# A two-layer relational graph attention kernel: the elu's exponential written to PSUM in the first aggregation, and the scores' turn placed behind five parts of the product in the last

## The chip, the cores and the metric

The kernel runs on one core of a Trainium2 chip. The metric is device time in microseconds (us) from the start to the end of one launch. A core has five engines with one instruction stream each: TensorE (PE in the profile; PEld are its weight loads), VectorE (DVE), ScalarE (ACT), GpSimd (POOL) and SyncE (SP). An engine takes its own instructions in the order in which the program wrote them; between engines only semaphores order the work.

## The reference

Two layers of relational graph attention run over 3125 nodes of 768 features and 53,125 edges of 3 types; a residual and a LayerNorm close it. Cut to what matters:

```python
def rgat_conv(x, W, q, k, b, src, dst, etype, heads, out_ch, n_nodes):
    xr = jnp.einsum('nd,rdf->rnf', x, W)
    oi, oj = xr[etype, dst], xr[etype, src]
    alpha = jax.nn.leaky_relu(oi @ q + oj @ k, 0.2)
    e = jnp.exp(alpha - segment_max(alpha, dst)[dst])
    a = e / (segment_sum(e, dst)[dst] + 1e-16)
    msg = a[:, :, None] * oj.reshape(-1, heads, out_ch)
    return segment_sum(msg.reshape(-1, heads * out_ch), dst) + b

h = elu(rgat_conv(x, W1, q1, k1, b1, src, dst, etype, 4, 192, n))
out = layernorm(x + rgat_conv(h, W2, q2, k2, b2, src, dst, etype, 1, 768, n))
```

elu(v) is max(v, 0) + min(exp(v), 1) - 1.

## The kernel before, in words

Edges are sorted by destination. The 3125 nodes make 25 blocks of up to 128; a block owns 17 slots of 128 edges (block 0 has 14). One slot is one gather: an indirect DMA that POOL issues (L485) and that brings 128 rows of 772 numbers from the table `ftab` in device memory into one row of a ring in SBUF. An aggregation makes 422 of them.

There are three stages. Phase 1 multiplies the nodes by the weights of layer 1 and writes the table. Phase 2 is the first aggregation (4 heads): scores (`alpha`), their transposition on PE, maxima by scans and exponentials, weighted sums of the rows on PE into PSUM, then `e_y`, `e_x`, `e_h` (the elu), the transposition of h (`e_t`, into the PSUM tile `pt`, the two "turning banks"), and the dense products of layer 2 (`po`), which refill the table. Phase 3 is the last aggregation (one head): for each block

- `a_alpha` (DVE L1309 to L1315) adds the rows' keys and the queries to scores `al`; it needs the block's last gathered row;
- `a_turn` turns `al` and `next` on PE into the bank `pa`;
- `a_scan` (DVE L1326, L1328, L1331) finds the maxima, `a_exp` (ACT L1335) takes the exponential, `a_back` turns it back on PE;
- `weigh` (DVE L1359, four instructions) multiplies the marks by it, and `sums` (8 groups on PE, into `acc`) adds the weighted rows;
- of the block before, the `r_` steps bring the sums together (`r_plus`, DVE L1420, two halves), and the product `D` by one relation's second weights runs on PE in 12 parts: six of 512 columns, then six of 256. LayerNorm and the store close it.

The order is not found by a scheduler. Both phases put each step into a list with a key, in units of one gather (17 of them are a block), sort the list, and call the steps in that order; so the keys decide what stands in front of what on each engine. `STEPS3["s"]` holds, counted from the unit e at which the block's gathers are issued: alpha, turn, scan, exp, back, weigh, sums. `STEPS3["r"]` holds the `r_` steps (the last two are the halves of `r_plus`), `STEPS3["d"]` the 12 parts. Two steps occur once, behind the last gather: for the last block the product runs in a split precision, and its weights are split there, `w2_high` (ACT L1427, six casts) and `w2_low` (DVE L1431, six subtractions), with keys 6.0 to 6.51 units after the last block's e, alternating:

```python
for t in range(DT):
    when(NK + 6 + 0.1 * t, w2_high, t)
    when(NK + 6.01 + 0.1 * t, w2_low, t)
```

In phase 2 the elu works on a 128x768 tile: `e_x` (ACT L1026) writes the exponential to `ey`, `e_h` (DVE L1063) clips it, and L1065 and L1066 add max(y, 0) to it.

Of the kernel before, what the change touches and what calls it, by code (L numbers as in the profile page):

```python
# [9 lines left out]
F32 = mybir.dt.float32  # L10
# [11 lines left out]
P = 128  # L22
# [43 lines left out]
def _index(ap):  # L66
# [36 lines left out]
STEPS3 = {"f": -13,  # L103
          "marks": -5,
          "q": (-19, -17.27, -3.5, -2),
          "s": (1.9, 3.0, 3.05, 3.1, 5.6, 5.7, 9.5),
          "round": 0.9,
          "r": (16.7, 16.7, 16.72, 16.75, 19.25, 19.3, 16.71, 16.73, 20.5, 20.6),
          "t": (16.74, 16.78),
          "d": ((19.5, 22.5, 7), (22.8, 26.2, 5)),  # L110
          "y": (26.6, 26.7, 26.8, 29.5, 29.6),
# [4 lines left out]
def kernel(  # L116
# [31 lines left out]
    F1 = D // H1  # L148
# [695 lines left out]
    def phase2(work, psum):  # L844
# [177 lines left out]

        def e_x(b):
            s = blk[b]
            s["ey"] = work.tile([P, 4, F1], F32, name="ey", bufs=1)
            S.activation(s["ey"], s["y"][:, :, :F1], AF.Exp)  # L1026

        def busy(n):
# [117 lines left out]
        for b in range(NB):  # L1146
            at_0 = base(b + 1) - SL
            when(max(at_0 + STEPS2["marks"], 0.5), marks, b)
            for u, name in enumerate(("first", "second")):
                when(max(at_0 + STEPS2["f"][u], 0.1 + 0.1 * u), f_load, b, u)  # L1150
                for d, f in zip(STEPS2[name], (alpha, turn, scan, back, weigh, sums)):
                    if b > 0:
                        when(at_0 + d, f, b, u)
                if b == 0:
                    for d, f in zip(STEPS2["second0" if u else name], (alpha, turn, scan, back, weigh, sums)):
                        if u == 1 or f is not sums:
                            when(d, f, b, u)
                    if u == 0:
                        for i, d in enumerate(STEPS2["sums0"]):
                            when(d, sums, b, u, i)  # L1160
            for d, f in zip(STEPS2["h"], (e_y, e_x, e_h, h_row, e_t, e_s, e_s2)):
                when(at_0 + d, f, b)
            n = 0
            for i, (a, e, m) in enumerate(STEPS2["d"]):
                for j in range(m):
                    when(at_0 + a + (e - a) * j / m, d_part, b)
                    n += 1
                    for p in range(4):
                        if n == 18 * (p + 1):
                            when(at_0 + a + (e - a) * j / m + STEPS2["copy"], d_row, b, p)  # L1170
                            when(at_0 + a + (e - a) * j / m + STEPS2["tail"], d_tail, b, p)
            assert n == 72
# [431 lines left out]
    with tc.manual_schedule():  # L1604
        with tc.tile_pool(name="share", bufs=1) as pool:
# [5 lines left out]
            with tc.tile_pool(name="wbuf", bufs=1) as wbuf:  # L1611
                weights[0] = [wbuf.tile([P, DT, WA], F32R, name=f"wa{s}") for s in "HL"]
                with tc.tile_pool(name="wrest", bufs=1) as wrest, tc.tile_pool(name="pre", bufs=1) as pre:
# [16 lines left out]
                    with tc.tile_pool(name="work0", bufs=1) as work, tc.tile_pool(  # L1630
                        name="psum0", bufs=1, space=PSUM
# [23 lines left out]
                    with tc.tile_pool(name="work1", bufs=1) as work, tc.tile_pool(  # L1655
                        name="psum1", bufs=1, space=PSUM
# [3 lines left out]
                with tc.tile_pool(name="exbuf", bufs=1) as exbuf:  # L1660
                    extra = exbuf.tile([P, NX, RW], F32, name="extra")
                    with tc.tile_pool(name="work2", bufs=1) as work, tc.tile_pool(
                        name="psum2", bufs=1, space=PSUM
                    ) as psum:
                        phase2(work, psum)
                    with tc.tile_pool(name="work3", bufs=1) as work, tc.tile_pool(
                        name="psum3", bufs=1, space=PSUM
# [545 lines left out]
```

## Time and profile before

| | us |
|---|---|
| median of 3 runs | 1728.38 |
| lowest, highest | 1726.51, 1731.38 |
| the profiled execution's own time | 1726.83 |
| its span in the profile | 1724.9 |
| phase 3's gathers, first start to last start | 1131.84 to 1681.86 |

Busy shares of the span: PE 95%, DVE 64%, POOL 52%, ACT 25%. They are averages over three stages with different limits, so the stages have to be read one by one: which engine has no idle time there, and what ended the idle time of the others. In a row of a timeline the first number is the start in us from the start of the span, the second the duration, and the bracket gives the idle time just before it and what ended it; rows that are alike and follow one another are put together with their count. PE's instructions overlap, so a duration of a group is less than the sum of its members.

### The profile page before, as it was taken

The page shows a single profiled execution, that of the slowest core. Times are in us where ns is not written, and L with a number is a line of the kernel's source. Part 1 is how long each engine was busy: PE and PEld are TensorE (multiplying, and loading weights), DVE is VectorE, ACT ScalarE, POOL GpSimd, SP SyncE. Part 2 cuts the span into 40 slices and gives each one's busy share as a digit, 9 for nine tenths or more (in the row PEclk, how much of TensorE's full clock was granted, in tenths as well). Part 3 has the DMA queues.
Part 4 walks back from the last instruction along what each step waited for, and adds up shares of the span by engine and source line. Part 5 has one row for each costly group of instructions (what it writes and reads, how often), then busy time and mean ns, then how long its engine had stood idle before and what let it go on. Part 6 is the DMA issues. An engine that isn't in the chain of part 4 may idle for free.

```text
span 1724.9 us, 39077 instructions
## 1 busy us (share of the span) xinstructions
PE 1640.5 (95%) x14233; PEld 1269.5 (74%) x14233; DVE 1106.6 (64%) x4107; ACT 423.8 (25%) x796; POOL 904.8 (52%) x907
## 2 busy tenths in 40 slices
PE   9999999999996999999999999939999999999996
PEld 8999999999995788888888888924444444444443
DVE  5467666676425566666677777465766666666665
ACT  5122222112110111111111111212333333333333
POOL 5100000000007777777777777057777777777770
PEclk9999999999997999999999999969999999999999
DMA  9576766666568999999999999569999999999991
GB/s 329 180 244 210 258 220 210 199 183 203 191 251 281 330 345 355 347 348 348 346 346 356 354 351 351 172 230 324 334 336 340 335 337 338 338 336 340 334 338 39
DMA packets 169368, 500.48 MB, mean 290 GB/s; under 512 B 39891, under 2 KB 82490, under 8 KB 169167
## 3 DMA queue, kind: packets, MB, share of 16 engines
q0 software_dynamic: 70832, 343.91, 56.1%
q1 hardware_dynamic: 90104, 143.89, 25.0%
q10 hardware_dynamic: 8230, 10.10, 1.7%
q8 instruction: 114, 1.87, 0.4%
q14 instruction: 88, 0.71, 0.1%
HBM read 412.96 MB, written 89.63 MB: 291 GB/s over the span
## 4 chain that ended last, share of the span: by engine, by line
PE 69%; DMA 12%; issue 8%; POOL 6%; DVE 4%; ACT 0%; POOLq 0%; DVEq 0%; ACTq 0%; SPq 0%
PE po L56 47%; PE acc L56 13%; PE D L56 4%; DMA waH<-ftab,ridx 3%; DMA waL<-ftab,ridx 3%; POOL waH L485 2%; PE pa L59 2%; PE pt L59 2%; DMA share<-ftab,ridx 1%; DMA extra<-ftab,ridx 1%; POOL waL L485 1%; POOL extra L485 1%; DMA spare_rows<-ftab,ridx 1%; POOL share L485 1%; PE bank L56 1%
## 5 line engine op out<-in xcount | busy, mean ns | idle before, releaser
L485 POOL DMA_INDIRECT extra<-ftab,ridx x296 | 303.3, 1025 | 90.2 <-issue 48.2
L56 PE MATMUL po<-waH,hT 128*128 128x386 f32 (+1 forms) x1200 | 323.1, 344 | 1.0 <-DVE hT L1055 0.8
L56 PE MATMUL po<-waH,xT 128*128 128x386 f32 x1104 | 293.0, 341 | 0.0
L485 POOL DMA_INDIRECT share<-ftab,ridx x209 | 214.2, 1025 | 63.7 <-issue 36.3
L56 PEld LDWEIGHTS po<-waH,hT 128*128 128x128 f32 x1200 | 220.4, 189 | 3.4 <-DVE hT L1055 1.1
L56 PE MATMUL po<-waL,hT 128*128 128x386 f32 (+1 forms) x600 | 207.6, 346 | 0.0
L56 PE MATMUL D<-extra,AT 128*128 128x512 f32 (+1 forms) x576 | 207.2, 503 | 0.0
L56 PEld LDWEIGHTS po<-waH,xT 128*128 128x128 f32 x1104 | 202.4, 189 | 0.5 <-issue 0.4
L56 PE MATMUL po<-waL,xT 128*128 128x386 f32 x552 | 186.9, 339 | 0.0
L598 ACT COPY share<-po 128x386 f32<-128x386 f32 x150 | 72.3, 482 | 371.2 <-PE po L56 298.7
L56 PEld LDWEIGHTS D<-extra,AT 128*128 128x128 f32 x576 | 105.6, 193 | 67.9 <-issue 60.3
L56 PE MATMUL acc<-waL,marks 128*32 128x386 f32 (+1 forms) x860 | 152.8, 490 | 0.0
L56 PE MATMUL po<-wbH,xT 128*128 128x386 f32 (+1 forms) x552 | 147.5, 341 | 1.3 <-DVE wbL L431 1.3
L56 PE MATMUL acc<-waH,marks 128*32 128x384 f32 (+1 forms) x828 | 141.3, 496 | 0.7 <-DVE marks L1359 0.7
L56 PE MATMUL acc<-extra,marks 128*32 128x386 f32 (+1 forms) x564 | 129.5, 487 | 0.0
L485 POOL DMA_INDIRECT waL<-ftab,ridx x108 | 108.1, 1001 | 32.9 <-issue 26.8
L56 PE MATMUL acc<-extra,sel 128*32 128x193 f32 x2736 | 122.6, 331 | 2.3 <-DVE sel L963 2.3
L927 ACT ACTIVATE e<-e 32x128 f32<-32x128 f32 (+2 forms) x50 | 15.5, 310 | 432.9 <-DVE e L926 432.9
L485 POOL DMA_INDIRECT waH<-ftab,ridx x103 | 102.8, 998 | 31.4 <-issue 25.0
L56 PEld LDWEIGHTS po<-waL,hT 128*128 128x128 f32 x600 | 113.7, 190 | 0.6 <-issue 0.3
L762 POOL DMA_DIRECT2D share<-in_L_gnn_W_dram x24 | 12.8, 536 | 188.4 <-DVE w2j L773 117.3
L56 PEld LDWEIGHTS acc<-extra,sel 128*32 128x32 f32 x2736 | 86.7, 111 | 31.4 <-issue 5.8
(312 smaller groups left out, 3078.1 us busy)
## 6 DMA issues: line engine op xcount, KB each, us to landing
ftab<-share SPq DMA_DIRECT2D x150, 193.0 KB
ftab<-r SPq DMA_DIRECT2D x50, 386.0 KB
sT<-dr_d SPq DMA_DIRECT2D x23, 544.0 KB
xb_d<-share SPq DMA_DIRECT2D x25, 384.0 KB
ftab<-y SPq DMA_DIRECT2D x100, 96.0 KB
share<-xb_d SPq DMA_DIRECT2D x25, 384.0 KB
share<-in_x_dram SPq DMA_DIRECT2D x24, 384.0 KB
out_dram<-share SPq DMA_DIRECT2D x24, 384.0 KB
```

The costliest lines, as they stand in the source:

```text
L56: return self.add(self.engine.matmul(to, weights, moving, **more), to, moving)
L59: return self.add(self.engine.transpose(to, a, unit), to, a)
L485: return G.indirect_dma_start(out=to, out_offset=None, in_=tab, in_offset=_index(i[:, j:j + 1]), bounds_check=NP * R - 1, oob_is_err=False)
L598: S.copy(o[:, :HW], po[:, :HW])
L762: G.dma_start(w2[i][p:p + n], l2["W"][r, at:at + n, :])
L927: S.activation(e, e, AF.Exp)
```

## The change

Two edits. In phase 2 the exponential of the elu goes into a PSUM tile of the name that `e_t` uses a little later for h's transposition (`pt`, one buffer, two banks), where it was a tile in SBUF; the three DVE instructions of `e_h` then read it from there. In phase 3 the scores' steps get later keys: alpha 1.9 to 2.3, turn 3.0 to 4.3, scan and exp with it, back 5.6 to 6.5, weigh 5.7 to 6.6; the sums keep 9.5. The second half of `r_plus` moves from 20.6 to 21.37, which is 4.37 in the next block's units.

```diff
 STEPS3 = {...
-          "s": (1.9, 3.0, 3.05, 3.1, 5.6, 5.7, 9.5),
+          "s": (2.3, 4.3, 4.35, 4.4, 6.5, 6.6, 9.5),
           "round": 0.9,
-          "r": (16.7, 16.7, 16.72, 16.75, 19.25, 19.3, 16.71, 16.73, 20.5, 20.6),
+          "r": (16.7, 16.7, 16.72, 16.75, 19.25, 19.3, 16.71, 16.73, 20.5, 21.37),
...
         def e_x(b):
             s = blk[b]
-            s["ey"] = work.tile([P, 4, F1], F32, name="ey", bufs=1)
+            ey = psum.tile([P, 2, 512], F32, name="pt", bufs=1)
+            s["ey"] = ey.rearrange("p c (w f) -> p (c w) f", w=2)[:, :, :F1]
             S.activation(s["ey"], s["y"][:, :, :F1], AF.Exp)
```

The order of instructions changes in phase 3 alone, on PE and DVE; POOL, SP and ACT keep theirs. PE around the turn of the last block (every block has this pattern; `pa<-fident,al` and `pa<-fident,next` are the turn, `pa<-fident,e` the turn back, the D rows the parts of the product), before:

```order
L56 MATMUL D_14329<-extra,AT 128x512 x2
L59 MATMUL pa<-fident,al_0_14262 17x128
L59 MATMUL pa<-fident,next_14264 17x2x64
L56 MATMUL D_14329<-extra,AT 128x512 x4
L56 MATMUL D_14330<-extra,AT 128x256
L59 MATMUL pa<-fident,e 128x17
L56 MATMUL D_14330<-extra,AT 128x256 x5
L56 MATMUL acc_20486<-waL,marks 32x384 x2
```

and after:

```order
L56 MATMUL D_14329<-extra,AT 128x512 x5
L59 MATMUL pa<-fident,al_0_14262 17x128
L59 MATMUL pa<-fident,next_14264 17x2x64
L56 MATMUL D_14329<-extra,AT 128x512
L56 MATMUL D_14330<-extra,AT 128x256 x3
L59 MATMUL pa<-fident,e 128x17
L56 MATMUL D_14330<-extra,AT 128x256 x3
L56 MATMUL acc_20486<-waL,marks 32x384 x2
```

The turn stands behind five parts, not two; between it and the turn back there are now one part of 512 and three of 256, where there were four of 512 and one of 256; behind the turn back three are left of five.

DVE in the last block, behind the scores (the rows that go to share from acc are the halves of `r_plus`, marks from marks and pa is `weigh`, L1431 is `w2_low`), before:

```order
L1326 SCALAR_TENSOR_TENSOR F<-f,pa 17x256
L1328 SCALAR_TENSOR_TENSOR B<-f,F 17x192
L1331 TENSOR_TENSOR e<-pa,B 17x128
L1420 SCALAR_TENSOR_TENSOR share<-acc_20261,half,share 128x768
L1420 SCALAR_TENSOR_TENSOR share<-acc_20260,half,share 128x768
L1359 TENSOR_TENSOR marks<-marks,pa 128x544
L1359 TENSOR_TENSOR marks<-marks,pa 128x128
L1359 TENSOR_TENSOR marks<-marks,pa 128x32
L1359 TENSOR_TENSOR marks<-marks,pa 128x256
L1431 TENSOR_TENSOR waH<-extra,waH 128x768 x5
L1431 TENSOR_TENSOR waL<-extra,waH 128x768
```

and after (line numbers are one higher):

```order
L1421 SCALAR_TENSOR_TENSOR share<-acc_20261,half,share 128x768
L1327 SCALAR_TENSOR_TENSOR F<-f,pa 17x256
L1329 SCALAR_TENSOR_TENSOR B<-f,F 17x192
L1332 TENSOR_TENSOR e<-pa,B 17x128
L1421 SCALAR_TENSOR_TENSOR share<-acc_20260,half,share 128x768
L1432 TENSOR_TENSOR waH<-extra,waH 128x768 x5
L1432 TENSOR_TENSOR waL<-extra,waH 128x768
L1360 TENSOR_TENSOR marks<-marks,pa 128x544
L1360 TENSOR_TENSOR marks<-marks,pa 128x128
L1360 TENSOR_TENSOR marks<-marks,pa 128x32
L1360 TENSOR_TENSOR marks<-marks,pa 128x256
```

In every block one half of `r_plus` now stands ahead of the scan and the other behind it. In the last block alone `weigh` has moved from ahead of the six subtractions to behind them.

## Rows read from the trace of the kernel before

**Rows 1.** What PE waited for in phase 3 (total, times, longest, in us).

```profile
PE pa L59 <- DVE al L1313: 22.3, 16, 3.7
```

**Rows 2.** POOL's timeline: the first and the last gather of phase 3.

```profile
1131.84 1.00 POOL L485 DMA_INDIRECT waH<-ftab,rfirst  x1 [48.63 <-DMA f<-ed_d]
...
1681.86 1.00 POOL L485 DMA_INDIRECT share<-ftab,ridx  x1 [0.30 <-issue]
```

**Rows 3.** Three blocks: us; PE, PEld, DVE, ACT, POOL busy; PE clock; DMA; GB/s.

```profile
1339.91:1360.88 20.97, 20.97 (x160) 9.98 (x160) 15.06 (x65) 7.92 (x13) 16.09 (x17) 1.00 0.94 333
1470.08:1493.76 23.68, 21.31 (x161) 9.90 (x160) 15.00 (x65) 7.92 (x13) 18.19 (x19) 1.00 0.95 335
1581.30:1606.26 24.96, 22.89 (x160) 10.55 (x160) 15.09 (x65) 7.92 (x13) 19.17 (x20) 0.93 0.94 338
```

**Rows 4.** Timeline around the turn of a block that waits (block 23).

```profile
1665.94 0.18 DVE L1313 SCALAR_TENSOR_TENSOR al<-a 128x17 f32<-128x17 f32 x1
...
1666.26 0.27 PE L59 MATMUL pa<-fident,al 128*17 128x128 f32 x1 [0.88 <-DVE al L1313]
...
1666.88 0.68 DVE L1326 TENSOR_TENSOR_SCAN F<-f,pa 17x256 f32<-17x256 f32 x1
...
1670.64 0.23 PE L59 MATMUL pa<-fident,e 17*128 17x17 f32 x1
```

**Rows 5.** Timeline of the last block, from its turn to its sums.

```profile
1687.43 0.27 PE L59 MATMUL pa<-fident,al 128*17 128x128 f32 x1
...
1687.65 4.03 PE L56 MATMUL D<-extra,AT 128*128 128x512 f32 x10
...
1689.14 0.28 DVE L1331 TENSOR_TENSOR e<-pa,B 17x128 f32<-17x128 f32 x1
1689.35 2.05 DVE L1420 SCALAR_TENSOR_TENSOR share<-acc,half,share 128x768 f32<-128x768 f32 x2
...
1689.67 4.48 ACT L1427 CAST waH<-extra 128x768 fp32r<-128x768 f32 x6
...
1691.61 0.23 PE L59 MATMUL pa<-fident,e 17*128 17x17 f32 x1
...
1691.88 1.34 DVE L1359 TENSOR_TENSOR marks<-marks,pa 128x544 f32<-128x544 f32 x4 [0.48 <-PE pa L59]
1693.14 4.42 DVE L1431 TENSOR_TENSOR waH<-extra,waH 128x768 fp32r<-128x768 f32 x5
1694.13 0.52 PE L56 MATMUL acc<-waL,marks 128*32 128x384 f32 x2
...
1697.49 0.95 DVE L1431 TENSOR_TENSOR waL<-extra,waH 128x768 fp32r<-128x768 f32 x1
```

**Rows 6.** PE's timeline: the closing product's start, behind the last block's sums.

```profile
1707.17 4.23 PE L56 MATMUL D<-waH,waL 128*128 128x512 f32 x17 [0.43 <-DVE waL L1457]
```

**Rows 7.** PE's timeline: turns that waited over 2 us.

```profile
1489.38 0.27 PE L59 MATMUL pa<-fident,al 128*17 128x128 f32 x1 [2.34 <-DVE al L1313]
...
1600.27 0.33 PE L59 MATMUL pa<-fident,al 128*17 128x128 f32 x1 [2.02 <-DVE al L1313]
```

**Rows 8.** DVE groups of phase 2 by shape: count, busy us, mean ns of one.

```profile
L1063 DVE TENSOR_SCALAR ey<-ey 128x768 f32<-128x768 f32 x25 | 14.3, 571 | 0.9 <-ACT ey L1026 0.9
...
L963 DVE TENSOR_TENSOR sel<-marks,pa 128x768 f32<-128x768 f32 x1 | 1.0, 953 | 1.7 <-PE pa L59 1.7
```

**Rows 9.** Timeline of one elu of phase 2: its last step, a gather, scores, turn.

```profile
837.02 0.96 DVE L1066 SCALAR_TENSOR_TENSOR y<-y,ey 128x768 f32<-128x768 f32 x1
...
837.21 1.64 POOL L485 DMA_INDIRECT share<-ftab,ridx  x1 [0.30 <-DVE y L1065]
...
838.70 0.17 DVE L902 SCALAR_TENSOR_TENSOR al<-a 128x32 f32<-128x32 f32 x1
...
840.80 0.29 PE L59 MATMUL pa<-fident,al 128*36 128x128 f32 x1
```

**Rows 10.** PE's timeline: its last wait in phase 2, near that stage's start.

```profile
602.18 0.27 PE L59 MATMUL pa<-fident,al 128*32 128x128 f32 x1 [0.98 <-DVE al L902]
```

## The prediction

> **What bounds the kernel now.** I read stage by stage what PE waited for, then the engine that PE waits for, then single blocks.
>
> In phase 2 the view of waits lists no wait of PE between 606 and 1125; its last one there is 0.98 us long, at 602.18 [rows 10]. Behind it that stage lasts as long as PE's own work, and faster work elsewhere is worth nothing.
>
> In phase 3 PE's turn waits 16 times for the scores, 22.3 us in all [rows 1]. The scores wait for the block's last gathered row, and POOL never rests: a gather takes 1.00 and the next starts 0.30 later, with "issue" as the reason [rows 2]. From the first start to the last it is 550.02 us for 421 intervals, 1.306 each; 17 of them are 22.2 us per block. PE's own work is 20.97 us in a block without a wait [rows 3]. So the supply of rows bounds phase 3, and PE's waits are the difference, 22.2 - 20.97 = about 1.2 per block, drawn in uneven portions. A later turn can't remove them: it puts work ahead of the wait that is then missing behind it. What it gives, it gives once, at the end.
>
> **The turn behind five parts.** Four parts of 512 and one of 256 take 4.03 us [rows 5], so a part of 512 is about 0.87, and three are 2.6. In a block whose turn waits, now, the scores start at 1665.94, the turn at 1666.26, the scan at 1666.88, the turn back at 1670.64 [rows 4]. From the turn back to the sums it is 2.52 in the last block (1691.61 to 1694.13 [rows 5]); so the sums come 4.38 + 2.52 = 6.9 behind the turn, 7.2 behind the scores' start, and PE has work all the while.
>
> After, three parts less lie between turn and sums: by PE's work alone the sums come 6.7 - 2.6 + 0.2 = 4.3 behind a turn that didn't wait (6.70 is the last block's 1687.43 to 1694.13 [rows 5]). DVE's chain there: e ends 1.99 behind the turn (1689.14 + 0.28 [rows 5]), the exponential at 2.3, the turn back runs at 2.46, the second half of `r_plus` (1.02, half of 2.05) ends at 3.0, and the four `weigh` instructions, 1.34 long, at 4.3. The two chains just meet; the wait is 0.2 at most. Where the turn waits, the first half of `r_plus` stands ahead of the scan: the scan then starts about 1.55 behind the scores' start instead of 0.94, since the 1.02 fills in part the time in which DVE waited for the turn. From the scan's start it is 1.55 to the end of e, 1.0 of `r_plus`, 1.34 of `weigh`: the sums come 5.4 behind the scores' start. PE waits about 0.55 at the turn back and 0.25 at the sums. Such a block gives its sums 7.2 - 5.4 = 1.8 earlier, and the next turn has 2.6 more work ahead of it. PE's need becomes 20.97 + 0.8 = 21.8, still under 22.2: the steady state stays with the supply, worth 0. The bounds: below, all waits go, -22.3; above, waits 0.6 longer than I make them in 22 blocks, 22 x (22.4 - 22.2) = 4.4.
>
> **The last block.** Its turn is late for PE's work, not for the scores; it goes from 1687.43 [rows 5] 2.6 later (parts) and 1.8 earlier (block 23's end), to 1688.2. There DVE now has the six subtractions `w2_low` ahead of `weigh`. They need the six casts, which ACT begins behind the exponential, at turn + 2.24 (1689.67); a cast is 4.48/6 = 0.75, so the first subtraction starts at turn + 3.1. Five of them take 1697.49 - 1693.14 = 4.35, the last 0.95 [rows 5]: they end at turn + 8.4. `weigh` takes 1.34 more: turn + 9.75. PE's parts end at turn + 4.2, and the first group of sums needs all four instructions of `weigh` (its slots lie in the first and the last piece of the marks). So the sums start at turn + 9.8, at 1698.0, against 1694.13: **+3.9 us** (from 3.2, where block 23 gives 2.5, to 4.8, where it gives 0.9). All behind it is one chain, the sums and then the closing product, which starts at 1707.17 and waits for what the sums' results become [rows 6]; it gets no shorter. The subtractions' results are used there first, so having them earlier gains nothing.
>
> **PE's clock.** In the last block PE is now idle for 9.8 - 4.2 = 5.6 us. At 1600.27 it had been idle for 2.02 us [rows 7], and the block around it had a mean granted clock of 0.93, so a part of it at 1.2 GHz, and 22.89 us of PE; the block with the 2.34 us of 1489.38 had 1.00 throughout, 2.4 GHz, and 21.31 [rows 3, 7]. An idle time of that length is not always followed by the low level; 22.89 - 21.31 = 1.6 is its price where it is. 5.6 is more than twice either, so I take it as paid once: **+1.6** (0 to 2.5, the upper end an estimate for sums and closing product both partly at the low level).
>
> **The exponential in PSUM.** The last instruction of `e_h` had two inputs in SBUF, and the gather beside it took 1.64 instead of 1.00 [rows 2, 9]; with one input in PSUM that 0.64 may go. It counts only up to PE's last wait, 0.98 at 602.18 [rows 10], ahead of which the ring is filled and refilled once: **-0.4** (0 to -1.0, the whole wait).
> The Trainium skill (SBUF — State Buffer, Who interferes with whom) says that a VectorE instruction with two SBUF inputs contends with a GpSimd instruction that reads SBUF, and that one with a single SBUF input outside the two-port modes does not. The 1.64 agrees with its first half; what the second half saves here is the same 0.64 a gather.
> Against the edit stands the clip, L1063: 0.571 from SBUF to SBUF, while an instruction of as many elements with an input in PSUM took 0.953 [rows 8]; so DVE has 0.4 more per block, ahead of the next scores and of h's transposition.
> The Trainium skill (VectorE: DVE Perf Modes, Why PSUM operands drop a tier) has this as a rule, fp32 with an operand in PSUM runs at the plain rate; the two rows agree, and by the rule alone, without the cover below, the sum would be 10 us higher.
> The cover: in the block shown the scores ended at 838.87 and PE's turn ran at 840.80 [rows 9], 1.9 later, so 0.4 costs 0 (if the cover were gone: 25 x 0.4 = 10).
>
> **Sum.** 3.9 + 1.6 - 0.4 = +5.1. The profiled execution (span 1724.9, 1726.83 with what lies around it) would go to 1731.9; it was 1.55 under the median of the runs, so on the median it is 1728.4 + 5.1 = **1733.5**. A measurement can tell about 0.3%, 5.2 us, from no change: the forecast lies at that edge.
>
> **The rivals.**
> First, the last block costs nothing, because `weigh` or the sums find a way past the subtractions; the turn's one gift stays: the sums come at 1688.2 + 4.4 = 1692.6, 1.5 earlier than 1694.13, and with the -0.4 it is 1726.5, no change. For it: the casts were early and the subtractions done at 1698.44 [rows 5], long before use. Against it: an engine keeps the order of its instructions. 0.11.
> Second, faster: the waits for the scores go, because PE and not the supply sets the pace; -22.3 and about three low-clock stretches of 1.6 less, 1701. It decides once POOL has idle time other than "issue". Against it: it has none in the rows read. 0.03.
> Third, faster: gathers without their 0.64 speed up phase 2, 25 x 0.64 = 16 at most, 1712. Against it: no wait of PE for 520 us. 0.03.
> Fourth, slower than I say: the new waits at the turn back and at the sums exceed 1.2 us a block, where I make them 0.8; from there on PE bounds phase 3 and each tenth costs 2.2 us. At 1.4 it is 5.1 + 4.4, 1738. For it: three chains meet within 0.2 us, and a low clock makes PE's side longer. Against it: all durations in these chains are those of the rows. 0.13.
>
> **How the numbers follow.** Forecast 0.70, its bounds 3.2 + 0 - 1.0 = +2.2 and 4.8 + 2.5 + 0 = +7.3, 1730.6 to 1735.7, and a microsecond or two to each side for gathers that other work stretches. The range, 1726 to 1737.5, takes in the first rival and the lower part of the fourth and leaves out some 0.2. Slower by over 0.3% (above 1733.6): 0.32 of the forecast's 0.70 and the fourth's 0.13: 0.45. Faster by over 0.3%: the second and third, 0.06. Within: 0.38 and the first's 0.11, 0.49.
>
> **What would show it.** Right: in the last block the six subtractions ahead of the four `weigh` rows, PE idle for about 5.6 us before its first sum, released by `weigh`, and a clock of 0.5 behind it; gathers of phase 3 still 1.30 apart, the last start within 2 us of 1681.86; fewer us of waits for scores, new ones of 0.2 to 0.6 at the turn back and the sums; the clip near 0.95; phase 2's blocks as long as before. Wrong: a first sum less than 8 us behind the last turn; a shorter phase 3 together with waits for scores gone; waits of PE between 606 and 1125.

## The result, and the profile after

| | us |
|---|---|
| median of before, 17 runs | 1728.19 (1725.15 to 1733.69) |
| median of after, 17 runs | 1730.85 (1729.5 to 1737.12) |
| ratio after / before | 1.0019, 95% interval 1.001 to 1.0028 |
| span of the profiled execution | 1724.9 before, 1727.6 after |

The change made the kernel slower by 0.19%, 3.3 us by the ratio (1.7 to 4.8 by its interval). The forecast was 1733.5, 5.1 more than before: the right sign, inside the range, too large by about two microseconds. The interval is narrower than the 0.3% that the prediction took for the least that can be told from no change: 0.19% is clear of zero.

In the last block six subtractions stand ahead of `weigh` on DVE, as the order had said. This is the timeline of after from the last turn on (it answers [rows 5]; line numbers are one higher):

```profile
1685.33 0.27 PE L59 MATMUL pa<-fident,al 128*17 128x128 f32 x1
...
1687.57 4.48 ACT L1428 CAST waH<-extra 128x768 fp32r<-128x768 f32 x6
...
1687.80 0.23 PE L59 MATMUL pa<-fident,e 17*128 17x17 f32 x1
...
1687.96 1.56 PE L56 MATMUL D<-extra,AT 128*128 128x256 f32 x6
...
1688.42 4.43 DVE L1432 TENSOR_TENSOR waH<-extra,waH 128x768 fp32r<-128x768 f32 x5 [0.17 <-ACT waH L1428]
...
1692.77 0.95 DVE L1432 TENSOR_TENSOR waL<-extra,waH 128x768 fp32r<-128x768 f32 x1
1693.64 1.34 DVE L1360 TENSOR_TENSOR marks<-marks,pa 128x544 f32<-128x544 f32 x4
1694.40 1.23 PE L56 MATMUL acc<-waL,marks 128*32 128x384 f32 x3 [4.88 <-DVE marks L1360]
...
1695.03 0.85 PE L56 MATMUL acc<-extra,marks 128*32 128x384 f32 x2
```

The turn back comes 2.47 behind the turn and needs no wait. The subtractions start at 1688.42, turn + 3.09, and `weigh` at turn + 8.31. The sums start at turn + 9.07, where before they started at turn + 6.70; the bracket gives 4.88 us of idle PE, ended by `weigh`. The rows of the first group that read `extra` go only at 1695.03, 0.63 later, when all of `weigh` is through (1693.64 + 1.34 = 1694.98).

Two windows show PE's clock behind that wait, after first and before second. Columns as in [rows 3]; the clock is the number ahead of the DMA share.

```profile
1694.40:1698.40 4.00, 4.00 (x27) 3.02 (x31) 3.40 (x12) 0.27 (x2) 0.00 (x0) 0.57 0.02 4
1694.40:1707.86 13.46, 12.68 (x121) 9.77 (x121) 4.08 (x16) 2.28 (x4) 0.00 (x0) 0.87 0.08 32
```

```profile
1694.13:1698.13 4.00, 4.00 (x53) 1.68 (x56) 4.00 (x5) 1.30 (x2) 0.00 (x0) 1.00 0.02 4
1694.13:1705.46 11.33, 10.54 (x121) 4.00 (x120) 7.79 (x18) 3.46 (x6) 0.00 (x0) 1.00 0.09 37
```

In the first 4 us of sums the mean clock was 0.57, so mostly 1.2 GHz, and half as many matmuls were done (27 records against 53). From the first sum to the closing transposition it took 13.46 instead of 11.33.

What PE waited for in phase 3, after (it answers [rows 1]), and the row on the exponential of before:

```profile
PE pa L59 <- DVE al L1314: 15.4, 12, 3.8
...
PE pa L59 <- ACT e L1336: 7.9, 16, 2.0
```

```profile
PE pa L59 <- ACT e L1335: 2.0, 1, 2.0
```

The waits for the scores fell by 6.9. Those for the exponential rose to 7.9, where before there was a single one of 2.0. Together they are 24.3 before and 23.3 after: the waits of phase 3 have changed their name and hardly their sum. POOL gave the same picture as in [rows 2], shifted:

```profile
1130.23 1.00 POOL L485 DMA_INDIRECT waH<-ftab,rfirst  x1 [49.60 <-DMA f<-ed_d]
...
1679.27 1.00 POOL L485 DMA_INDIRECT share<-ftab,ridx  x1 [0.30 <-DMA out_dram<-share]
```

First to last start is 549.04, 0.98 less than the 550.02 before; the profiles of the experiments, those on a slower chip apart, lie between 548.91 and 550.24, so 0.98 is within their scatter. The first gather came 1.61 earlier, 0.51 of which was there already at the first gather of phase 2.

In phase 2, groups of DVE by shape (they answer [rows 8] and [rows 9]):

```profile
L1064 DVE TENSOR_SCALAR pt<-pt 128x768 f32<-128x768 f32 x25 | 24.0, 958 | 0.9 <-ACT pt L1027 0.9
L1067 DVE SCALAR_TENSOR_TENSOR y<-y,pt 128x768 f32<-128x768 f32 x25 | 23.8, 953 | 0.9
```

```profile
835.41 0.95 DVE L1067 SCALAR_TENSOR_TENSOR y<-y,pt 128x768 f32<-128x768 f32 x1
835.54 1.00 POOL L485 DMA_INDIRECT extra<-ftab,ridx  x1 [0.30 <-DVE y L1066]
```

The clip takes 0.958 instead of 0.571, and the gather beside the last step takes 1.00 where it took 1.64. It is so throughout: in the 22 blocks of after in which a gather runs beside this step, it took 0.99 or 1.00, and before it took up to 1.79.

So the spans of before and after differ by these pieces, all worked out from starts in the two profiles: start of phase 2 -0.51, up to the first gather of phase 3 -1.10 more, the gathers -0.98, last gather to last turn +0.49 (5.57 to 6.06), turn to first sum +2.37, first sum to closing transposition +2.13; together +2.4, and 0.3 in what follows PE's last instruction.

### The profile page after: what moved, and what is told of

Its sections match the earlier page's. It is cut to its first block, busy times and chain, and to the rows that moved or that the text cites. A ratio compares the mean times of both kernels' runs of the same rounds, so it can differ in the third digit from the quotient of the medians.

```text
span 1727.6 us, 39066 instructions
## 1 busy us (share of the span) xinstructions
PE 1639.7 (95%) x14233; PEld 1344.3 (78%) x14233; DVE 1118.3 (65%) x4107; ACT 421.8 (24%) x796; POOL 896.4 (52%) x907
## 4 chain that ended last, share of the span: by engine, by line
PE 76%; DMA 9%; issue 6%; DVE 4%; POOL 4%; ACT 1%; POOLq 0%; DVEq 0%; ACTq 0%; SPq 0%
PE po L56 47%; PE acc L56 19%; PE D L56 4%; DMA waL<-ftab,ridx 2%; DMA waH<-ftab,ridx 2%; PE pa L59 2%; POOL waH L485 2%; PE pt L59 2%; DMA extra<-ftab,ridx 1%; DMA share<-ftab,ridx 1%; POOL waL L485 1%; DVE share L1421 1%; PE bank L56 1%; POOL share L485 1%; DMA share<-ftab,rfirst 1%
## 5 line engine op out<-in xcount | busy, mean ns | idle before, releaser
L485 POOL DMA_INDIRECT extra<-ftab,ridx x296 | 298.9, 1010 | 92.7 <-issue 51.2
L56 PE MATMUL D<-extra,AT 128*128 128x512 f32 (+1 forms) x576 | 202.6, 494 | 0.0
```

The source lines that it names most:

```text
L56: return self.add(self.engine.matmul(to, weights, moving, **more), to, moving)
L485: return G.indirect_dma_start(out=to, out_offset=None, in_=tab, in_offset=_index(i[:, j:j + 1]), bounds_check=NP * R - 1, oob_is_err=False)
```

## The experiments

All ratios are to the kernel before, run on the same chip in the same rounds, with 95% intervals. My theory is that the slowdown is the last block's order on DVE and what follows from it on PE, while the gathers set the pace of the rest. The rivals are that the later turn itself costs, that the clip in PSUM costs, and that PE and not the supply bounds phase 3.

**Each edit alone.** a_only takes the keys back; b_only takes the PSUM tile back.

```diff
-          "s": (2.3, 4.3, 4.35, 4.4, 6.5, 6.6, 9.5),
+          "s": (1.9, 3.0, 3.05, 3.1, 5.6, 5.7, 9.5),
...
-          "r": (16.7, 16.7, 16.72, 16.75, 19.25, 19.3, 16.71, 16.73, 20.5, 21.37),
+          "r": (16.7, 16.7, 16.72, 16.75, 19.25, 19.3, 16.71, 16.73, 20.5, 20.6),
```

> The kernel before with the first edit alone (exponential in PSUM; keys of the last aggregation as before). My theory: phase 2 loses its last wait and the gathers beside the elu take 1.00 instead of 1.6; PE bounds phase 2 behind 602, so it is worth 0.5 to 2.5 us once: -1.1 us, phase 3's first gather about 1.1 earlier, ratio 0.9985 to 0.9997; the clip at 0.95 hidden. Rival: the slower clip (0.4 a block) is on the path: +1 to +10 us, and PE waits in phase 2.

```diff
-            ey = psum.tile([P, 2, 512], F32, name="pt", bufs=1)
-            s["ey"] = ey.rearrange("p c (w f) -> p (c w) f", w=2)[:, :, :F1]
+            s["ey"] = work.tile([P, 4, F1], F32, name="ey", bufs=1)
```

> The kernel before with the second edit alone (the later keys). My theory: all of the changed kernel's loss is here, in the last block (sums 9.1 behind the turn, PE idle 4.9, then 1.2 GHz): +3.8 us (2.5 to 5), phase 3's gathers still 1.30 apart. Rival: the edit costs nothing and the loss comes from the first one: -1 to 0.

Measured: a_only 0.9998 (0.9986 to 1.0009), -0.3 us and within the noise; b_only 1.0025 (1.0014 to 1.0035), +4.3 us. The whole loss is in the later keys. In a_only the clip lasts 0.959, as in after, and costs nothing that shows; the rival on it falls. The last block of b_only is that of the changed kernel, sums 9.07 behind the turn with an idle time of 4.87, but from there to the closing transposition it took 14.26, not 13.46. The window (columns as above) has the low clock for the whole of the first 4 us:

```profile
1701.58:1705.58 4.00, 4.00 (x25) 2.38 (x29) 3.40 (x12) 0.27 (x2) 0.00 (x0) 0.50 0.02 4
```

**The subtractions behind `weigh`.** One key of the changed kernel:

```diff
-            when(NK + 6.01 + 0.1 * t, w2_low, t)
+            when(NK + 6.61 + 0.1 * t, w2_low, t)
```

> The changed kernel with the six subtractions w2_low at keys 6.61 to 7.11, behind weigh (the casts stay at 6.0 to 6.5). My theory: the last block's sums come 4.1 behind its turn instead of 9.07 and PE stays at 2.4 GHz: -4.95 - 2.1 = -7 against the changed kernel, so -4.4 against before, about 1723.8, ratio 0.997 to 0.998. Rival (the subtractions cost nothing there, the end is set elsewhere): as the changed kernel, +2.7.

Measured: 1725.6 against 1728.85, ratio 0.9979 (0.9968 to 0.999), 3.6 us faster than before. Its last block in the timeline:

```profile
1693.30 0.27 PE L59 MATMUL pa<-fident,al 128*17 128x128 f32 x1
...
1696.14 1.32 DVE L1360 TENSOR_TENSOR marks<-marks,pa 128x544 f32<-128x544 f32 x4
1697.40 4.42 DVE L1432 TENSOR_TENSOR waH<-extra,waH 128x768 fp32r<-128x768 f32 x5
1697.42 0.52 PE L56 MATMUL acc<-waL,marks 128*32 128x384 f32 x2
```

The sums start 4.12 behind the turn without a listed wait; from there to the closing transposition it is 11.41 and the records show no low clock in between. Against the changed kernel the two ratios give 0.9979 / 1.0019 = 0.996, 6.9 us, for -7 expected. The one key is the whole difference between a slower and a faster kernel.

**The subtractions ahead of `weigh`, in the kernel before.** The keys of the casts go along, since a subtraction needs its cast; on ACT the casts still stand right behind the exponential. The turn, the scan and `r_plus` keep their keys:

```diff
-            when(NK + 6 + 0.1 * t, w2_high, t)
-            when(NK + 6.01 + 0.1 * t, w2_low, t)
+            when(NK + 5.61 + 0.01 * t, w2_high, t)
+            when(NK + 5.611 + 0.01 * t, w2_low, t)
```

> The kernel before with one thing alone: casts and subtractions get keys 5.61 to 5.67, so that on DVE the six subtractions stand ahead of weigh in the last block; turn, scan and r_plus as before. My theory: sums 9.1 behind the turn instead of 6.7, +2.4; PE then idles 2.4 us, after which the clock may or may not fall: +2.4 to +4.5 (ratio 1.0014 to 1.0026). Rival (the later turn is what costs in the changed kernel, not the subtractions): 0.

> low_first again, on the same footing. The first look had the subtractions start 3.88 behind the turn (both halves of r_plus stand ahead of them), the sums 9.86 behind it, and 13.57 from there to the closing transposition. My theory: here the same, 9.86 - 6.70 = +3.2 and 13.57 - 11.34 = +2.2, together +5.4, ratio 1.0025 to 1.0035. Rival (the later turn costs, not the subtractions): 0.

The first of the two ran on another chip, on which the kernel before takes 1985 us (last section): 1.0015 (0.9997 to 1.0034), with sums 9.86 behind the turn. The second: 1.0021 (1.0012 to 1.003), 1731.77 against 1727.6, +3.6 us. So with the old turn the new order on DVE alone makes the kernel as slow as the change did, and the rival that the later turn costs falls. In the trace of low_first_2 both halves of `r_plus` stand ahead of the subtractions:

```profile
1686.80 0.27 PE L59 MATMUL pa<-fident,al 128*17 128x128 f32 x1
...
1690.68 4.42 DVE L1431 TENSOR_TENSOR waH<-extra,waH 128x768 fp32r<-128x768 f32 x5
...
1695.88 1.34 DVE L1359 TENSOR_TENSOR marks<-marks,pa 128x544 f32<-128x544 f32 x4
1696.66 1.03 PE L56 MATMUL acc<-waL,marks 128*32 128x384 f32 x4 [3.09 <-DVE marks L1359]
```

The mechanism is there as expected: sums 9.86 behind the turn, an idle time of 3.09, and 13.63 to the closing transposition, where 13.57 was expected. Against before that is +3.16 and +2.30, together 5.5, and the runs show 3.6 (2.1 to 5.2), under the ratio that was expected. The whole profiled execution took 4.9 longer than that of before (1731.69 against 1726.83), which is within the interval.

**The wait kept, PE kept busy.** In the changed kernel, behind the last turn back, PE gets extra multiplications of 128 columns whose results are not used:

```diff
+        def last_busy(n):
+            for _ in range(n):
+                T.matmul(bank[:, :P], ident, ident, start=True, stop=True)
...
+        when(NK + 9.4, last_busy, 40)
```

> The changed kernel with 40 more multiplications of 128 columns (results unused) on PE in the last block, between the turn back and the sums, so that PE is not idle while it waits for weigh. My theory: the sums start where they did, about 9.1 behind the turn, but run at 2.4 GHz: 2.1 less than the changed kernel, +0.6 against before. Rival (the sums take 13.5 instead of 11.3 because weigh's pieces come late, not because of the clock): +2.7, as the changed kernel.

With 40 it was a poor experiment: they outlasted the wait by far, the sums came 13.05 behind the turn, and the ratio is 1.0033 (1.0018 to 1.0048). But from there the sums took 11.33, as before the change. With 20:

> As busy_gap with 20 multiplications instead of 40 (there they took 0.21 each and outlasted the wait; the sums came 13.05 behind the turn and then took 11.34 to the closing transposition, not 13.45). My theory: sums about 9.1 behind the turn, 11.34 long: 2.1 less than the changed kernel, about +0.6 against before, ratio 0.9995 to 1.001. Rival (the low level comes whatever PE does): +2.7.

> busy_gap20 again: sums 9.1 behind the turn, from there 11.4 to 12 to the closing transposition instead of 13.45, so 1.5 to 2.1 under the changed kernel: +0.6 to +1.8 against before, ratio 1.0003 to 1.001. Rival (the low level comes whatever PE does): +2.7 to +3.3.

On the slower chip 1.0017 (1.0003 to 1.003), again 1.0017 (1.0007 to 1.0026) for the second, 1729.56 us. Timeline and windows of busy_gap20_2:

```profile
1698.37 1.34 DVE L1360 TENSOR_TENSOR marks<-marks,pa 128x544 f32<-128x544 f32 x4
1699.14 1.03 PE L56 MATMUL acc<-waL,marks 128*32 128x384 f32 x4 [0.41 <-DVE marks L1360]
```

```profile
1699.14:1703.14 4.00, 4.00 (x47) 2.76 (x51) 3.40 (x12) 0.27 (x2) 0.00 (x0) 1.00 0.00 0
1699.14:1711.08 11.94, 11.16 (x120) 7.26 (x121) 4.08 (x16) 2.28 (x4) 0.00 (x0) 1.00 0.09 36
```

PE is idle for 0.41 instead of 4.88 and the clock stays at 1.00, 2.4 GHz; the sums start 9.07 behind the turn as in after. From there it is 11.94: so of the 2.13 that after loses behind its first sum, 1.52 are the clock and 0.6 are `weigh`'s later pieces, for which the first group stops. The trace confirms the price of the clock. It is not the same each time: beside these 11.94 it was 1.52 in after, 1.69 in low_first_2, 2.06 in less_pe_2 (below; 14.00 behind an idle time of 5.59) and 2.32 in b_only.

The times of the runs do not confirm it: 1.0017 is no better than the changed kernel's 1.0019, where 1.0003 to 1.001 was expected. With intervals of 0.001 to each side 1.5 us can hide. One source of scatter shows: four of the eleven runs, the profiled one among them, took 1732.8 to 1734.0 and the other seven 1728.1 to 1729.9, and in the profiled one the first gather of phase 2 came at 523.67, 4.0 later than in before, behind work that no edit touches. From that gather to the closing transposition it took 1.6 more than in before; in after it was 2.9 more.

Of every run the mean clock of the whole span is on record too. With the later keys and the idle time it was on average 0.9798 in the changed kernel (17 runs) and 0.9799 in b_only (12), and with the later keys but without the idle time 0.9815 in busy_gap20_2 (11) and 0.9813 in low_last (12). By the window, 4 us at 0.57 lower such a mean by 0.001, so this points to a price that is paid in most runs. It doesn't prove it: busy_gap, whose PE was kept busy as well, had 0.9803 (12 runs), and one mean doesn't say where the clock fell.

**Without the first edit.** low_last with `ey` in SBUF, the diff of b_only:

> The later keys with the subtractions behind weigh, but the exponential in SBUF as before: what the first edit is worth beside low_last. My theory: the first edit gives 0.4 (0 to 1.1), so this one is 3.2 below before (2.5 to 4), ratio 0.9977 to 0.9986. Rival (the first edit gives all of low_last's gain): 0.

> b_low_last again: low_last without the first edit. low_last was at 0.9979 of before. My theory: the first edit gives 0.4 (0 to 1.1), so this one is at 0.998 to 0.9988 and phase 3's first gather comes 0 to 1 us later than with it. Rival (the first edit gives all of the gain): 1.0.

On the slower chip 0.999 (0.9977 to 1.0003); the second 0.9982 (0.9973 to 0.9991), 1724.92 us against 1727.6. Beside low_last's 0.9979 that leaves the exponential in PSUM 0.0003, 0.5 us, with both intervals far wider. The gain of low_last is thus that of the later keys. Its traces show only a part of it at the end: from the last gather to the closing transposition it is 23.60 before, 22.04 in low_last and 22.88 in b_low_last_2. Where the rest of the 3.1 to 3.6 us comes from is not shown.

**PE with less work in phase 3.** Half of the six 256-column parts is left out in all blocks but the last:

```diff
                 for t in range(DT):
+                    n = min(n, 512 if f == 0 else 128)
                     T.matmul(to[:, :n], s["AT"][:, t * P:(t + 1) * P], w2[:, t, f:f + n], start=(t == 0),
```

> The changed kernel with half of the product's six 256-column parts left out in all blocks but the last (columns 640 to 767 are not computed there): PE has 6 x 0.21 = 1.3 us less per block. My theory (the gathers bound phase 3): first to last gather stays 549 to 550 us, the waits for scores and for the exponential grow by 1.2 to 1.3 a block, about 28 us in all, and the time falls by 0 to 3 us. Rival (PE bounds phase 3, its waits are of its own making): 24 x 1.3 = 31 us less, phase 3's gathers 520 us.

> less_pe again (columns 640 to 767 of the product are not computed in all blocks but the last), beside the kernel before with gathers at full pace: the first look was on a chip on which the kernel before took 1985 us, phase 3's gathers 793 to 807. My theory (the gathers bound phase 3): 549 to 550 us from its first gather to its last, PE's waits longer by about 1.3 a block, the time 0 to 3 us under the changed kernel. Rival (PE bounds phase 3): 31 us less, gathers 520 us.

The first ran on the slower chip, 2005.7 us in a single run; there it says little. (The 793 to 807 named with the second are counted from within phase 2; from the first gather of phase 3 it was 653 to 668.) The second: 1731.02 us, 1.0017 (1.0007 to 1.0028), the changed kernel's own ratio. Its gathers:

```profile
1131.08 1.00 POOL L485 DMA_INDIRECT waH<-ftab,rfirst  x1 [49.63 <-DMA ftab<-r]
...
1680.16 1.00 POOL L485 DMA_INDIRECT share<-ftab,ridx  x1 [0.30 <-issue]
```

549.08 us, against 549.04 in after. What it waited for in phase 3, and a window over 20 blocks, less_pe_2 first, then after's window:

```profile
PE pa L59 <- ACT e L1336: 23.2, 25, 2.0
PE pa L59 <- DVE al L1314: 13.4, 13, 3.8
```

```profile
1227.69:1670.64 442.95, 413.02 (x3175) 250.35 (x3171) 300.00 (x1296) 156.57 (x260) 339.29 (x340) 1.00 0.95 339
```

```profile
1227.69:1670.64 442.95, 426.56 (x3184) 260.38 (x3180) 301.12 (x1298) 156.50 (x260) 339.29 (x341) 1.00 0.95 339
```

In these 20 blocks the product's parts of 256 columns, now of 128, took 25.1 us less, 0.21 for each of the 120 parts, as was put down; groups of PE by shape, after first:

```profile
L56 PE MATMUL D<-extra,AT 128*128 128x256 f32 x240 | 60.4, 388 | 0.0
L56 PE MATMUL D<-extra,AT 128*128 128x128 f32 x240 | 35.3, 283 | 0.0
```

PE's busy time fell by only 13.5, mostly because the sums took 8.4 more (213.8 to 222.2): their first group starts earlier and then stops for the last piece of `weigh`, and such a stop counts as busy (behind the turn back of 1291.28 the group starts at 1292.49 and goes on at 1293.12, `weigh` being through at 1293.06). The listed waits of all of phase 3 grew from 23.3 to 36.6. The time that was freed became waiting, listed or not, and not a microsecond came out at the end. That the gathers bound phase 3 is shown.

## Why the prediction was right, point by point

**Where the time is.** Right on both stages. Phase 2 after lists one wait of PE between 606 and 1125, which the prediction had named as a sign of being wrong, but it is of 0.2 us, and the 0.4 of DVE per block in the clip is hidden. Phase 3 is bound by its gathers (less_pe_2), and a turn that comes later removed no waits there, it turned 6.9 us of waits for scores into 5.9 of waits for the exponential. One sign of being right was missed: the last gather started 2.59 before 1681.86, not within 2; that is the 0.51, 1.10 and 0.98 of the list above.

**The turn behind five parts.** The turn back at + 2.46 was measured at 2.47; the sums of a block whose turn doesn't wait at + 4.3 were at 4.12 in the last block of low_last, since PE's parts and `weigh` meet without a wait. The new wait of 0.55 at the turn back shows as 5.9 us in 15 blocks, 0.4 each.

**The last block.** Sums at turn + 9.8 and PE idle for 5.6: measured 9.07 and 4.88, because the step "the first group needs all four instructions of `weigh`" failed by half. The first matmuls need the first piece alone and start 0.76 behind it; the others of the group stop until the fourth piece is done, which gives back 0.6 of the 0.73 (11.94 against 11.33 with the clock held up). Counted like that the term is 9.67 - 6.70 = 2.97 beside the predicted 3.1. The turn's own shift, +0.8 predicted from 1687.43 to 1688.2, was -2.1 in the profile, but there everything ahead of it was earlier too; from the last gather to the last turn it is 5.57 before, 6.06 after, and between 6.42 and 7.35 in b_only, low_last, busy_gap, busy_gap20_2, less_pe_2 and b_low_last_2, so +0.5 to +1.8. With the old keys it was 5.47 in a_only and 6.27 in low_first_2, so 0.8 of that is scatter: that the predicted 0.8 lies inside is no test of how it was derived.

**The clock.** 1.6 predicted, 1.52 by after against busy_gap20_2, and 1.5 to 2.3 over the four profiled executions with a long idle time. The price came from one block in which the clock had fallen, and that it hit 1.52 so closely is in part luck.

**The exponential in PSUM.** -0.4 predicted. From the first gather of phase 2 to the first of phase 3 it took 612.17, 611.08, 611.69 and 612.40 without the edit (before, b_only, low_first_2, b_low_last_2) and 611.24, 611.08, 611.80, 611.65, 610.65 and 611.21 with it (a_only, after, low_last, less_pe_2, busy_gap20_2, busy_gap): means 611.84 and 611.27, 0.6 apart with a scatter of the same size. The runs don't tell it from zero.

**The sum.** From the last gather to the closing transposition 3.9 + 1.6 = 5.5 was predicted, and after's trace has 28.59 against 23.60, +5.0. Ahead of the last gather -0.4 was predicted, and the trace has -2.6 (0.51, 1.10 and 0.98), so that the two profiled executions differ by 2.9 (1729.69 against 1726.83), close to the 3.3 of the runs. But most of that -2.6 is within the scatter of single executions: from the first gather of phase 2 to the last gather of phase 3 the ten profiled executions, those on the slower chip apart, took 1160.0 to 1162.2 (1161.0 and 1161.1 in a_only and low_first_2, which have the old keys), and the one of before was the longest. The forecast is thus some two microseconds above the runs, and so was that for low_first_2. Which term was too large stays open: only the profiled execution has a timeline, and a time alone doesn't tell the end of a run from its beginning.

**Of the rivals** the first, that nothing is lost in the last block, fell with the listed wait of 4.88. Its time, 1.9 under before, is what the later turn gives when the subtractions are out of the way; low_last measures 3.6 (1.7 to 5.5) and b_low_last_2, without the first edit, 3.1 (1.6 to 4.7), so the gift of the turn may have been too small in it, but both intervals reach down to it. The second and third fell with less_pe_2 and a_only. The fourth asked for 1.2 us of new waits in a block; there were 0.4.

## What to carry to other kernels

Where a list of keys sets the order, a step that moves by a unit passes everything that has a key in between, once-only steps too: here six subtractions whose results nobody needed for another 15 us came to stand ahead of an instruction for which PE waited, in one block of 25, and turned a gain of 3.6 us into a loss of 3.3. So read the order at the ends of a loop as well as in its steady state, where work that is done once lies. And before a wait is hidden behind more work, look for what sets the rate of the thing that is waited for: the wait only takes another name.

## What the runs showed that I had not expected

- The kernel before took a median of 1728 us in three sets of runs and 1985 us in the fourth, on another chip. There phase 3's gathers took 653 us from first to last start (low_first) instead of 549 to 550, and POOL's gathers no longer ran back to back; two of its rows from the timeline of low_first, with idle times of 1.97 and 2.48 ahead of them:

```profile
1512.22 1.00 POOL L485 DMA_INDIRECT extra<-ftab,ridx  x1 [1.97 <-remote]
...
1525.87 1.00 POOL L485 DMA_INDIRECT share<-ftab,ridx  x1 [2.48 <-PE D L59]
```

The ratios kept their sign there (low_first 1.0015, then 1.0021 here; b_low_last 0.999, then 0.9982), but their intervals are wider and reach 1.
- An idle time of PE of 3.09 us (low_first_2) and of 4.88 us (after) was followed by the low clock, and so was one of 2.02 (1600.27 in [rows 7]; the block had 0.93 [rows 3]); one of 2.34 [rows 7] was not, so the length alone did not decide it. The sums behind the wait that was filled with unused multiplications ran at 1.00.
